# Scan kernel on one core: gate products on GpSimd from a copy of y, maxima joined three to one, and B split in a layout of 128 x 64

## The chip, the cores and the metric

The kernel runs on one core of a Trainium2 chip. Its time is device time in microseconds (us) of one launch; the figure used is the median of three runs. Five engines work in parallel, each through its own queue in order: TensorE (PE, with its weight loads as PEld), VectorE (DVE), ScalarE (ACT), GpSimd (POOL) and SyncE (SP), which here only issues DMAs.

## The reference, cut to what matters

The input x is (16, 96, 64, 64). Two blocks follow each other.

The first block works on windows of 8 x 8 pixels: a 1 x 1 convolution, then for each of the 64 nodes of a window its 9 nearest nodes by cosine distance, then an edge network and a maximum over the neighbours:

```python
feat = concat([x_i, x_j - x_i])                  # K = 9 neighbours j of node i
h = gelu((feat @ ew.T + eb) * es + et)           # O = 192 channels
h = max over the 9 neighbours
y = affine(conv1x1(h, fc2_w, fc2_b), fc2_s, fc2_t) + x
```

The second block is a state space model over the 4096 pixels of an image, in two layers, with D = 192 channels and 16 states:

```python
xs, z = split(layernorm(seq) @ in_w)
xc = silu(causal_conv4(xs));  dt, Bm, Cm = split(xc @ xproj_w)
delta = softplus(dt @ dt_w + dt_b)
h[l] = exp(delta * A) * h[l-1] + delta * Bm[l] * xc[l]    # per channel and state
y = sum over states of h * Cm  +  Dp * xc
seq = seq + (y * silu(z)) @ out_w                          # y * silu(z): "the gate"
```

A fusion product, a normalisation over the batch and the residual end it.

## The kernel before, in words

An image is cut into 8 rows of 512 pixels (a row of 8 windows). An *item* is one row of one layer of one image: 16 x 2 x 8 = 256 items. An item has 8 *steps* p = 0 to 7; each handles two of the 16 states for all 192 channels, as a tile of 128 partitions (64 channels for each of two states) by 3 x 512 columns. A step is

- ACT: `da` = exp(delta * A) in three instructions (L681), made two steps ahead, in one of four buffers `das`;
- PE: `bt`, the row of B of each state spread over 64 partitions by a selection matrix `bsel` (L702). B is held in `bparts` as three bfloat16 parts, whose sum is B;
- DVE: `db` = `u` * `bt` in PSUM (L707), the carry from the row before added into its first column (L852, from `first`), then the scan `hb` (L861);
- POOL: the last state kept (L886), then `hb` = `hb` * C (L887);
- PE: `hb` folded into `y` in PSUM (L718, L720), over all eight steps of the item. `y` has one buffer, in two tiles `ya` (512 columns) and `yb` (256).

All order is written out by hand: a loop over the 2048 steps issues the scan of a step, advances several generators by one yield each, then issues the next `db` and the fold of the step before. Engines follow this order in their queues. The generators, each running beside the steps:

- `norm(n+2)` from p = 0 and `prelude(n+2)` from p = 4 of item n make the inputs of the item after next (`xc`, `z`, `dbl`, `bparts`, `delta`, `u`). In `prelude`, the product `pd` gives dt, B and C in `dbl`; B appears three times in it, in partitions 0, 64 and 96 and up. ACT copies it to `dbl` and as bfloat16 to `bparts` (L612, L613); POOL subtracts (L640), ACT casts the difference (L647), POOL subtracts again (L657). Between these POOL has softplus' sums (L642, L644, L646) and the product for `u` (L652); DMAs then double `delta` and `u` over the partitions (L663, L665). Row C goes to DRAM (L616) and is read back spread over 64 partitions as `ct` (L674).
- `carry(n+1)` from p = 5 makes `first` on POOL and ACT (L690, L692, L696).
- `nearest` (every other item) and `edges` (one over two items) do the first block for later rows. `edges` makes one-hot matrices `oh` (L404 on POOL, L406 and L407 on ACT), products (L438, L441) and gelus (L446) into a buffer of `das`: three tiles of 128 x 512 for a pair of windows. `most` (L382) reduces each over its 8 neighbours; the nodes' own values `sa`, `sb` (L463, L475) join by two maxima (L859), and `fc2` follows (`product` in `edges`).
- `tail(n-1)` at p = 6 multiplies the gated `z` by `out_w` and updates `seq`.

The maxima wait in lists: `most` is put in `later[1]`, two steps on in `between`, and one is taken ahead of a scan where nothing else is, another behind the scan at p = 4 and 5; what is left goes out ahead of the maxima in `late`. The gates of item n-1 are issued on DVE at p = 1 of item n, around the addition of the carry:

```python
acts = opening + (gates(n - 1, y) if p == 1 and n else [])
...
if len(acts) > 1:
    acts.pop(0)()
if k:
    nc.vector.tensor_tensor(db[:, :, 0], db[:, :, 0], carried[n][:, :, p], ALU.add)
for act in acts:
    act()
```

Of the kernel before, what the change touches and what calls it, by code (L numbers as in the profile page):

```python
# [10 lines left out]
F32 = mybir.dt.float32  # L11
# [10 lines left out]
def tile_conv_knn_mamba(ctx: ExitStack, tc: tile.TileContext, w: dict, out: bass.AP):  # L22
# [8 lines left out]
    nc = tc.nc  # L31
# [127 lines left out]
    DT0 = 2 * NS  # L159
    PARTS = (0, 64, 96)  # L160
    ONE0 = PARTS[2] + NS
    bsel = const.tile([128, NPR, 128], BF16, name="bsel")
# [12 lines left out]
    NDA = 4  # L175
    das = [const.tile([128, NB3, Q], F32, name=f"da{i}") for i in range(NDA)]
    zeros = const.tile([128, NB3], F32, name="zeros")
    nc.vector.memset(zeros, 0.0)
# [15 lines left out]
    with tc.tile_pool(name="setup", bufs=2) as sp, tc.tile_pool(name="setup_ps", bufs=2, space=PSUM) as spp:  # L194
        for i in range(NL):
# [34 lines left out]
            nc.vector.memset(xp, 0.0)  # L230
            for r, src, n in ((0, R, 2 * NS), (DT0, 0, R), (PARTS[1], R, NS), (PARTS[2], R, NS)):
                nc.vector.tensor_copy(xp[:, :, r : r + n], xr[:, :, src : src + n])
# [147 lines left out]
    def most(out, g, at):  # L380

        nc.vector.tensor_reduce(out, g, AX.X, ALU.max)  # L382
        if at is not None:
            free.append(at)

    def edges(b, q):
# [4 lines left out]
        for hf in range(2):  # L391
# [29 lines left out]
            if hf == 0:  # L421


                hqa = pr.tile([128, Q], F32, tag="hqa", name=f"hqa_{nm}", bufs=1)
                hqb = pr.tile([128, QH], F32, tag="hqb", name=f"hqb_{nm}", bufs=1)
                hqa4 = hqa.rearrange("p (r w c) -> p w r c", r=WS, w=NW)
                hqb4 = hqb.rearrange("p (r w c) -> p w r c", r=WS, w=NP)


            for p in range(2):  # L430
                ohw = [ohs[p][:, h].rearrange("j i k -> j (i k)") for h in range(2)]
                at = free.popleft()
                g3 = das[at]
                unset.add(at)
                for part in range(3):
                    t = pm.tile([128, Q], F32, tag="mm", name=f"t_{nm}_{hf}_{p}_{part}")
                    if part < 2:
                        nc.tensor.matmul(t, lhsT=vus[p][:, part, :128], rhs=ohw[part], start=True, stop=True)  # L438
                    else:
                        for h in range(2):  # L440
                            nc.tensor.matmul(  # L441
                                t[half(h)], lhsT=vus[p][:, h, 128:], rhs=ohw[h], start=True, stop=True
                            )
                    g = g3[:, part, :]
                    j = part // 2
                    nc.scalar.activation(g, t, AF.Gelu, bias=e_b[:, j : j + 1], scale=e_s[:, j : j + 1])  # L446
                    w2 = 2 * hf + p
                    later[1].append(
                        partial(
                            most,  # L450
                            hqb4[:, w2] if part == 2 else hqa4[:, 2 * w2 + part],
                            g.rearrange("p (r c k) -> p r c k", r=WS, k=KO),
                            at if part == 2 else None,
                        )
                    )
                if p == 0:
                    yield TABLE
            if hf == 1:
# [3 lines left out]
                sa = pr.tile([128, Q], F32, tag="sa", name=f"sa_{nm}", bufs=1)  # L462
                nc.scalar.activation(  # L463
                    sa.rearrange("p (r w c) -> p r w c", r=WS, w=NW),
                    t.rearrange("p (w r c) -> p r w c", r=WS, w=NW),
                    AF.Gelu,
# [5 lines left out]
                for h in range(2):  # L472
                    nc.tensor.matmul(t[half(h)], lhsT=ew1[:, 128:], rhs=y4[:, h], start=True, stop=True)
                sb = pr.tile([128, QH], F32, tag="sb", name=f"sb_{nm}", bufs=1)
                nc.scalar.activation(  # L475
                    sb.rearrange("p (r w c) -> p r w c", r=WS, w=NP),
                    t.rearrange("p (w r c) -> p r w c", r=WS, w=NP),
                    AF.Gelu,
# [6 lines left out]

        late.append(partial(nc.vector.tensor_tensor, hqa, hqa, sa, ALU.max))
        late.append(partial(nc.vector.tensor_tensor, hqb, hqb, sb, ALU.max))
        yield
# [3 lines left out]
        def product():  # L492
            pf = pm.tile([C, Q], F32, tag="mm", name=f"pf2_{nm}")
            nc.tensor.matmul(pf, lhsT=fc2T[:, 0, :], rhs=hqa, start=True, stop=False)
            pf4 = pf.rearrange("o (r p h c) -> o h r p c", r=WS, h=2, c=WS)
            for h in range(2):
                nc.tensor.matmul(
                    pf4[:, h],
                    lhsT=fc2T[:, 1 + h, :],
                    rhs=hqb.rearrange("k (r p c) -> k r p c", r=WS, c=WS),  # L500
                    start=False,
                    stop=False,
                )
            nc.tensor.matmul(pf, lhsT=ident[:C, :C], rhs=xr, start=False, stop=True)
            return pf
# [37 lines left out]
    made = {}  # L543
    carried = {}

    def norm(n):
# [22 lines left out]
    def prelude(n):  # L569
# [5 lines left out]
        xc = pr.tile([128, Q + QH], F32, tag="xc", name=f"xc_{nm}")  # L575
        z = pr.tile([128, Q + QH], F32, tag="z", name=f"z_{nm}", bufs=4)

# [26 lines left out]
        yield  # L604
        bp = bparts[n % 2]
        ps = pm.tile([ONE0, Q], F32, tag="mm", name=f"pd_{nm}")
# [5 lines left out]
        nc.scalar.copy(dbl[:ONE0], ps)  # L612
        nc.scalar.copy(bp[:ONE0], ps)  # L613
        yield
        c_d = dram.tile([NS, Q], F32, tag="c_d", name=f"cd_{nm}")
        nc.sync.dma_start(out=c_d, in_=dbl[NS : 2 * NS, :])  # L616
# [21 lines left out]
        nc.scalar.activation(s1, s1, AF.Identity, bias=neg1)  # L638

        nc.gpsimd.tensor_tensor(dbl[PARTS[1] : ONE0], dbl[PARTS[1] : ONE0], bp[PARTS[1] : ONE0], ALU.subtract)  # L640
        yield
        nc.gpsimd.tensor_tensor(e, e, s1, ALU.subtract)  # L642
        yield
        nc.gpsimd.tensor_tensor(ln, ln, e, ALU.add)  # L644
        yield
        nc.gpsimd.tensor_tensor(ln, ln, rl, ALU.add)  # L646
        nc.scalar.copy(bp[PARTS[1] : ONE0], dbl[PARTS[1] : ONE0])  # L647
        yield
# [6 lines left out]
        doubled(u, s1)  # L655

        nc.gpsimd.tensor_tensor(bp[PARTS[2] : ONE0], dbl[PARTS[2] : ONE0], bp[PARTS[2] : ONE0], ALU.subtract)  # L657

# [51 lines left out]
    def folded(n, p, hb, y):  # L710

        i = items[n][1]
        xc = made[n][0]
        if p == 0:
            nc.tensor.matmul(y[0], lhsT=dp_diag[i][:, 0, :], rhs=xc[:, :Q], start=True, stop=False)
            nc.tensor.matmul(y[1], lhsT=dp_diag[i][:, 1, :], rhs=xc[:, Q:], start=True, stop=False)
        for h in range(2):
            nc.tensor.matmul(y[0][half(h)], lhsT=fold, rhs=hb[:, h, :], start=False, stop=(p == NPR - 1))  # L718
        for h in range(2):
            nc.tensor.matmul(  # L720
                y[1][half(h)], lhsT=fold, rhs=hb[:, 2, bass.ts(h, QH)], start=False, stop=(p == NPR - 1)
            )

    def gates(n, y):
        z = made[n][1]
        return [
            partial(nc.vector.tensor_tensor, z[:, cols], z[:, cols], part, ALU.mult)
            for cols, part in zip((slice(0, Q), slice(Q, Q + QH)), y)
        ]

    def tail(n):
# [3 lines left out]
        seq = seqs[b, k]  # L735
        z = made[n][1]

        def product():
            po = pm.tile([C, Q], F32, tag="mm", name=f"pow_{nm}")
            nc.tensor.matmul(po, lhsT=out_w[i][:, 0, :], rhs=z[:, :Q], start=True, stop=False)  # L740
            for h in range(2):
                nc.tensor.matmul(
                    po[:, bass.ts(h, QH)], lhsT=out_w[i][:, 1 + h, :], rhs=z[:, Q:], start=False, stop=False
                )
            nc.tensor.matmul(po, lhsT=ident[:C, :C], rhs=seq, start=False, stop=True)
            return po

# [67 lines left out]
    for m, (n, p) in enumerate(order):  # L815
# [27 lines left out]
        while uses:  # L843
            uses.pop(0)()
        acts = opening + (gates(n - 1, y) if p == 1 and n else [])
        opening.clear()
# [14 lines left out]
        nc.vector.tensor_tensor_scan(*(t.rearrange("p c q -> p (c q)") for t in (hb, das[at], db)), 0.0, ALU.mult, ALU.add)  # L861
        free.append(at)
        if p == 6 and n:
            going.append(tail(n - 1))
# [13 lines left out]
        if behind is not None:  # L878
            if p == 1:
                y = [  # L880
                    py.tile([128, Q], F32, tag="ya", name=f"ya_{nm}"),
                    py.tile([128, QH], F32, tag="yb", name=f"yb_{nm}"),
                ]
# [3 lines left out]
        nc.gpsimd.tensor_tensor(hb, hb, ct.unsqueeze(1).to_broadcast([128, NB3, Q]), ALU.mult)  # L887
        behind = (n, p, hb)
        while not held and len(soon) < AHEAD and coming:
            ahead()  # L890
    folded(*behind, y)
    for act in gates(NI - 1, y):
        act()
    drain(*going, tail(NI - 1))
# [50 lines left out]
```

## Time and profile before

| what | value |
| --- | --- |
| median of 3 runs | 13199.09 us (13182.12 to 13199.22) |
| span of the profiled execution | 13206.7 us |
| DVE busy | 12215.5 us, 92% |
| POOL busy | 11455.2 us, 87% |
| PE busy | 11033.5 us, 84% |
| ACT busy | 10512.7 us, 80% |
| mean granted TensorE clock | 0.959 |
| DMA, share of 16 engines in the SP queue | 33.1% |

The profiled execution has no time of its own beside its span; the span is 7.6 us (0.06%) over the median of the runs. In a group line the columns are line, engine, operation, output <- input, shapes and count, then busy us and mean ns of one, then the idle time of the engine ahead of them and who ended it. In a timeline line they are start, duration, engine, line, operation, tiles and shapes; in brackets stands the idle time ahead of it and its releaser.

### The profile page before, as it was taken

The numbers are of one execution on the slowest core, as the hardware profiler recorded it, in microseconds if no ns is written. First come the engines' busy times: TensorE is split into PE (matmuls) and PEld (weight loads), VectorE is DVE, ScalarE is ACT, GpSimd is POOL, SyncE is SP. The second block draws the span as 40 slices with busy tenths as digits, with TensorE's granted clock in tenths as the row PEclk, the third lists the DMA queues.
The fourth block names the chain that finished last, engine by engine and source line by source line (L and its number), as shares of the span: only waits on it lengthen the run. The fifth ranks groups of instructions, "written<-read, shape, count | busy, mean of one in ns | idle before, by whom it ended". The sixth has DMA issues, their size and how long they took to land.

```text
span 13206.7 us, 155165 instructions
## 1 busy us (share of the span) xinstructions
PE 11033.5 (84%) x46663; PEld 4408.0 (33%) x46664; DVE 12215.5 (92%) x9981; ACT 10512.7 (80%) x16401; POOL 11455.2 (87%) x7591
## 2 busy tenths in 40 slices
PE   6788888888888888888888888888888888888871
PEld 2233333333333333333333333333333333333320
DVE  2699999999999999999999999999999999999993
ACT  4688888888888888888888888888888888888762
POOL 1798999989999999999999899999999999998881
PEclk8899999999999999999999999999999999999985
DMA  1233333333333333333333333333333333333337
GB/s 27 72 86 91 91 91 86 92 91 86 92 88 93 87 90 94 89 88 91 91 90 87 91 92 87 90 92 91 85 94 89 90 88 90 93 88 90 84 89 237
DMA packets 887099, 1205.74 MB, mean 91 GB/s; under 512 B 282272, under 2 KB 413742, under 8 KB 877040
## 3 DMA queue, kind: packets, MB, share of 16 engines
q1 hardware_dynamic: 871792, 1169.34, 33.1%
q10 hardware_dynamic: 14464, 26.48, 0.6%
q8 instruction: 367, 6.01, 0.2%
q14 instruction: 476, 3.90, 0.1%
HBM read 706.82 MB, written 85.72 MB: 60 GB/s over the span
## 4 chain that ended last, share of the span: by engine, by line
DVE 30%; POOL 19%; PE 18%; ACT 14%; DMA 7%; issue 7%; SPq 4%; POOLq 0%; DVEq 0%; ACTq 0%
DVE hb L861 18%; POOL hb L887 12%; DVE db L707 9%; ACT da L681 5%; PE ya L718 3%; DMA ct<-cd 2%; SPq L663 2%; PE t L441 2%; PE t L438 1%; PE pj L584 1%; SPq L665 1%; PE yb L720 1%; PE bt L702 1%; PE pdta L622 1%; SPq L674 1%
## 5 line engine op out<-in xcount | busy, mean ns | idle before, releaser
L887 POOL TENSOR_TENSOR hb<-hb,ct 128x1536 f32<-128x1536 f32 x2048 | 7069.8, 3452 | 388.7 <-PE yb L720 87.9
L861 DVE TENSOR_TENSOR_SCAN hb<-da,db 128x1536 f32<-128x1536 f32 x2048 | 6859.6, 3349 | 108.3 <-ACT da L681 20.0
L681 ACT ACTIVATE da<-delta,a 128x511 f32<-128x511 f32 x6144 | 3940.0, 713 | 67.8 <-DVE hb L861 59.1
L707 DVE TENSOR_TENSOR db<-u,bt 128x1536 f32<-128x1536 f32 x2048 | 3602.9, 1759 | 170.0 <-PE pdtb L625 47.4
L718 PE MATMUL ya<-hb,fold 128*64 128x512 f32 x8192 | 2248.8, 628 | 220.9 <-POOL hb L887 215.2
L446 ACT ACTIVATE da<-t,eb,es 128x512 f32<-128x512 f32 x1536 | 1173.1, 777 | 778.9 <-PE t L438 518.7
L702 PE MATMUL bt<-bparts,bsel 128*128 128x512 bf16 x2047 | 797.5, 390 | 806.7 <-DVE db L707 745.8
L720 PE MATMUL yb<-hb,fold 128*64 128x256 f32 x8192 | 1265.6, 388 | 0.0
L720 PEld LDWEIGHTS yb<-hb,fold 128*64 128x64 f32 x8192 | 604.2, 141 | 1231.5 <-issue 1231.5
L438 PE MATMUL t<-oh,vu 128*128 128x512 f32 x2048 | 993.2, 607 | 23.3 <-ACT da L446 23.3
L584 PE MATMUL pj<-hn,conv_in 128*128 128x512 f32 x2048 | 930.9, 597 | 9.8 <-POOL hn L567 9.8
L718 PEld LDWEIGHTS ya<-hb,fold 128*64 128x64 f32 x8192 | 491.0, 139 | 1313.9 <-issue 552.2
L404 POOL TENSOR_SCALAR oh<-idb,node 64x1024 f32<-64x1024 uint16 x256 | 731.2, 2856 | 131.1 <-DMA idb<-idxd 131.1
L886 POOL COPY state<-hb 128x3 f32<-128x3 f32 x1792 | 342.1, 191 | 571.7 <-DVE hb L861 428.1
L441 PE MATMUL t<-oh,vu 128*64 128x512 f32 x2048 | 572.1, 638 | 302.1 <-ACT da L446 299.0
L382 DVE TENSOR_REDUCE hqa<-da 128x64 f32<-128x512 f32 x1024 | 677.0, 671 | 149.2 <-ACT da L446 149.1
L415 PE MATMUL pv<-ewT,y 96*64 96x192 f32 x2048 | 458.9, 349 | 248.6 <-ACT rs L564 166.0
L438 PEld LDWEIGHTS t<-oh,vu 128*128 128x128 f32 x2048 | 395.7, 195 | 465.3 <-issue 265.9
L596 ACT ACTIVATE xc<-pj,conv_b 128x512 f32<-128x512 f32 (+1 forms) x512 | 297.6, 581 | 289.6 <-PE pj L589 183.6
L584 PEld LDWEIGHTS pj<-hn,conv_in 128*128 128x128 f32 x2048 | 395.7, 193 | 395.0 <-issue 374.5
L589 PE MATMUL pj<-hn,conv_in 128*64 128x256 f32 x4096 | 498.9, 385 | 0.0
L415 PEld LDWEIGHTS pv<-ewT,y 96*64 96x64 f32 x2048 | 246.2, 140 | 696.9 <-ACT rs L564 268.6
(188 smaller groups left out, 18447.0 us busy)
## 6 DMA issues: line engine op xcount, KB each, us to landing
ct<-cd SPq DMA_DIRECT2D x4096, 128.0 KB
delta<-ln SPq DMA_DIRECT2D x1024, 128.0 KB
u<-s SPq DMA_DIRECT2D x1024, 128.0 KB
idb<-idxd SPq DMA_DIRECT2D x256, 256.0 KB
delta<-ln SPq DMA_DIRECT2D x1024, 64.0 KB
u<-s SPq DMA_DIRECT2D x1024, 64.0 KB
x<-in_x SPq DMA_DIRECT2D x128, 192.0 KB
rn<-r4d SPq DMA_DIRECT2D x128, 192.0 KB
```

The lines of the kernel that those rows point to most:

```text
L404: nc.gpsimd.tensor_scalar(ohj, numbers, node, None, ALU.is_equal)
L438: nc.tensor.matmul(t, lhsT=vus[p][:, part, :128], rhs=ohw[part], start=True, stop=True)
L441: nc.tensor.matmul(t[half(h)], lhsT=vus[p][:, h, 128:], rhs=ohw[h], start=True, stop=True)
L446: nc.scalar.activation(g, t, AF.Gelu, bias=e_b[:, j : j + 1], scale=e_s[:, j : j + 1])
L584: nc.tensor.matmul(ps, lhsT=wt[:, t, :128], rhs=hn[:, off : off + Q], start=(t == 0), stop=(t == taps - 1))
L681: nc.scalar.activation(da[:, c, 1:Q], delta[:, c, 1:], AF.Exp, scale=a_neg[i][:, c, p : p + 1])
L702: nc.tensor.matmul(bt, lhsT=bsel[:, p, :], rhs=made[n][2], start=True, stop=True)
L707: nc.vector.tensor_tensor(db, made[n][5], bt.unsqueeze(1).to_broadcast([128, NB3, Q]), ALU.mult)
L718: nc.tensor.matmul(y[0][half(h)], lhsT=fold, rhs=hb[:, h, :], start=False, stop=(p == NPR - 1))
L720: nc.tensor.matmul(y[1][half(h)], lhsT=fold, rhs=hb[:, 2, bass.ts(h, QH)], start=False, stop=(p == NPR - 1))
L861: nc.vector.tensor_tensor_scan(*(t.rearrange("p c q -> p (c q)") for t in (hb, das[at], db)), 0.0, ALU.mult, ALU.add)
L887: nc.gpsimd.tensor_tensor(hb, hb, ct.unsqueeze(1).to_broadcast([128, NB3, Q]), ALU.mult)
```

## The change

**Gates.** `y` becomes one tile of 128 x 2 x 512. Behind the scan at p = 1, ACT copies 768 columns of it from PSUM to a buffer of a ring of four `zs`; behind the product of that step, one POOL instruction of 128 x 768 multiplies the copy by `z`. `tail` reads the copy. The two DVE products go.

**Maxima.** The three reductions of 512 columns of a window pair become one of 1536, and the two maxima with `sa` and `sb` become one of 768. The result `hq` keeps the order of windows, and `fc2` reads it with other strides, in five products instead of four.

**B's parts.** `pd` holds B once. A DMA lays B's 16 rows of 512 out as 128 rows of 64; POOL makes the three bfloat16 parts there in five instructions; three DMAs put them in `bparts`. The two ACT casts and the two POOL subtractions go.

```diff
-    PARTS = (0, 64, 96)
-    ONE0 = PARTS[2] + NS
+    PARTS = (0, 32, 64)
+    ONE0 = DT0 + R
+    SEG = 128 // NS
+    QS = Q // SEG
...
+    zs = deque(const.tile([128, Q + QH], F32, name=f"z{i}") for i in range(4))
...
     def most(out, g, at):
-        nc.vector.tensor_reduce(out, g, AX.X, ALU.max)
-        if at is not None:
-            free.append(at)
+        nc.vector.tensor_reduce(out, g.rearrange("p s (i k) -> p s i k", k=KO), AX.X, ALU.max)
+        free.append(at)
...
-                    w2 = 2 * hf + p
-                    later[1].append(
-                        partial(
-                            most,
-                            hqb4[:, w2] if part == 2 else hqa4[:, 2 * w2 + part],
-                            g.rearrange("p (r c k) -> p r c k", r=WS, k=KO),
-                            at if part == 2 else None,
-                        )
-                    )
+                later[1].append(partial(most, hq[:, 2 * hf + p], g3, at))
...
-        late.append(partial(nc.vector.tensor_tensor, hqa, hqa, sa, ALU.max))
-        late.append(partial(nc.vector.tensor_tensor, hqb, hqb, sb, ALU.max))
+        late.append(partial(nc.vector.tensor_tensor, hq, hq, sa, ALU.max))
...
+            nc.tensor.matmul(pf, lhsT=ident[:C, :C], rhs=xr, start=True, stop=False)
+            pf5 = pf.rearrange("o (r w h c) -> o h w r c", r=WS, h=2, c=WS)
             for h in range(2):
+                for part, wt in ((h, 0), (2, 1 + h)):
+                    nc.tensor.matmul(
+                        pf5[:, h],
+                        lhsT=fc2T[:, wt, :],
+                        rhs=hq[:, :, part].rearrange("k w (r c) -> k w r c", c=WS),
...
         nc.scalar.copy(dbl[:ONE0], ps)
-        nc.scalar.copy(bp[:ONE0], ps)
         yield
+        bs = pr.tile([128, QS], F32, tag="bs", name=f"bs_{nm}", bufs=1)
+        nc.sync.dma_start(out=bs, in_=dbl[:NS, :])
...
-        nc.gpsimd.tensor_tensor(dbl[PARTS[1] : ONE0], dbl[PARTS[1] : ONE0], bp[PARTS[1] : ONE0], ALU.subtract)
+        b3 = pr.tile([128, 3, QS], BF16, tag="b3", name=f"b3_{nm}")
+        for part in range(3):
+            nc.gpsimd.tensor_copy(b3[:, part], bs)
+            if part < 2:
+                nc.gpsimd.tensor_tensor(bs, bs, b3[:, part], ALU.subtract)
         yield
+        bp = bparts[n % 2]
+        for r, part in zip(PARTS, range(3)):
+            nc.sync.dma_start(out=bp[r : r + NS], in_=b3[:, part])
...
-        nc.scalar.copy(bp[PARTS[1] : ONE0], dbl[PARTS[1] : ONE0])
...
-        nc.gpsimd.tensor_tensor(bp[PARTS[2] : ONE0], dbl[PARTS[2] : ONE0], bp[PARTS[2] : ONE0], ALU.subtract)
...
+    def emptied(n, y):
+        yc = zs.popleft()
+        nc.scalar.copy(yc, y.rearrange("p s q -> p (s q)")[:, : Q + QH])
+        return yc
+
+    def gate(n, yc):
         z = made[n][1]
-        return [
-            partial(nc.vector.tensor_tensor, z[:, cols], z[:, cols], part, ALU.mult)
-            for cols, part in zip((slice(0, Q), slice(Q, Q + QH)), y)
-        ]
+        nc.gpsimd.tensor_tensor(yc, yc, z, ALU.mult)
+        zs.append(z)
+        gated[n] = yc
...
-        acts = opening + (gates(n - 1, y) if p == 1 and n else [])
+        acts = list(opening)
...
         free.append(at)
+        if p == 1 and n:
+            yc = emptied(n - 1, y)
...
         nc.gpsimd.tensor_tensor(hb, hb, ct.unsqueeze(1).to_broadcast([128, NB3, Q]), ALU.mult)
+        if p == 1 and n:
+            gate(n - 1, yc)
```

More of the change, by code (lines that the diff above doesn't have):

```diff
@@ L230, in tile_conv_knn_mamba @@
             nc.vector.memset(xp, 0.0)
-            for r, src, n in ((0, R, 2 * NS), (DT0, 0, R), (PARTS[1], R, NS), (PARTS[2], R, NS)):
+            for r, src, n in ((0, R, 2 * NS), (DT0, 0, R)):
                 nc.vector.tensor_copy(xp[:, :, r : r + n], xr[:, :, src : src + n])
@@ L421, in edges @@
             if hf == 0:
[L424 to L427, printed above, removed]
+                hq = pr.tile([128, NP, NB3, NN], F32, tag="hq", name=f"hq_{nm}", bufs=1)
             for p in range(2):
@@ L461, in edges @@
                 nc.tensor.matmul(t, lhsT=ew1[:, :128], rhs=y, start=True, stop=True)
-                sa = pr.tile([128, Q], F32, tag="sa", name=f"sa_{nm}", bufs=1)
+                sa = pr.tile([128, NP, NB3, NN], F32, tag="sa", name=f"sa_{nm}", bufs=1)
                 nc.scalar.activation(
-                    sa.rearrange("p (r w c) -> p r w c", r=WS, w=NW),
-                    t.rearrange("p (w r c) -> p r w c", r=WS, w=NW),
+                    sa[:, :, 0:2],
+                    t.rearrange("p (w h i) -> p w h i", w=NP, h=2),
                     AF.Gelu,
@@ L473, in edges @@
                     nc.tensor.matmul(t[half(h)], lhsT=ew1[:, 128:], rhs=y4[:, h], start=True, stop=True)
[L474 removed]
                 nc.scalar.activation(
[L476 to L477 removed]
+                    sa[:, :, 2],
+                    t.rearrange("p (w i) -> p w i", w=NP),
                     AF.Gelu,
@@ L493, in product @@
             pf = pm.tile([C, Q], F32, tag="mm", name=f"pf2_{nm}")
-            nc.tensor.matmul(pf, lhsT=fc2T[:, 0, :], rhs=hqa, start=True, stop=False)
-            pf4 = pf.rearrange("o (r p h c) -> o h r p c", r=WS, h=2, c=WS)
+            nc.tensor.matmul(pf, lhsT=ident[:C, :C], rhs=xr, start=True, stop=False)
+            pf5 = pf.rearrange("o (r w h c) -> o h w r c", r=WS, h=2, c=WS)
             for h in range(2):
[L497 to L504, printed above, removed]
+                for part, wt in ((h, 0), (2, 1 + h)):
[3 more added lines that the diff above has]
+                        rhs=hq[:, :, part].rearrange("k w (r c) -> k w r c", c=WS),
+                        start=False,
+                        stop=h == 1 and part == 2,
+                    )
             return pf
@@ L544, in tile_conv_knn_mamba @@
     carried = {}
+    gated = {}
     def norm(n):
@@ L575, in prelude @@
         xc = pr.tile([128, Q + QH], F32, tag="xc", name=f"xc_{nm}")
-        z = pr.tile([128, Q + QH], F32, tag="z", name=f"z_{nm}", bufs=4)
+        z = zs.popleft()
         def project(wt, taps, part, out, bias):
@@ L604, in prelude @@
         yield
-        bp = bparts[n % 2]
         ps = pm.tile([ONE0, Q], F32, tag="mm", name=f"pd_{nm}")
@@ L714, in folded @@
         if p == 0:
-            nc.tensor.matmul(y[0], lhsT=dp_diag[i][:, 0, :], rhs=xc[:, :Q], start=True, stop=False)
-            nc.tensor.matmul(y[1], lhsT=dp_diag[i][:, 1, :], rhs=xc[:, Q:], start=True, stop=False)
+            nc.tensor.matmul(y[:, 0], lhsT=dp_diag[i][:, 0, :], rhs=xc[:, :Q], start=True, stop=False)
+            nc.tensor.matmul(y[:, 1, :QH], lhsT=dp_diag[i][:, 1, :], rhs=xc[:, Q:], start=True, stop=False)
         for h in range(2):
-            nc.tensor.matmul(y[0][half(h)], lhsT=fold, rhs=hb[:, h, :], start=False, stop=(p == NPR - 1))
+            nc.tensor.matmul(y[half(h), 0], lhsT=fold, rhs=hb[:, h, :], start=False, stop=(p == NPR - 1))
         for h in range(2):
             nc.tensor.matmul(
-                y[1][half(h)], lhsT=fold, rhs=hb[:, 2, bass.ts(h, QH)], start=False, stop=(p == NPR - 1)
+                y[half(h), 1, :QH], lhsT=fold, rhs=hb[:, 2, bass.ts(h, QH)], start=False, stop=(p == NPR - 1)
             )
-    def gates(n, y):
+    def emptied(n, y):
[3 more added lines that the diff above has]
+    def gate(n, yc):
         z = made[n][1]
-        return [
-            partial(nc.vector.tensor_tensor, z[:, cols], z[:, cols], part, ALU.mult)
-            for cols, part in zip((slice(0, Q), slice(Q, Q + QH)), y)
-        ]
+        nc.gpsimd.tensor_tensor(yc, yc, z, ALU.mult)
+        zs.append(z)
+        gated[n] = yc
     def tail(n):
@@ L735, in tail @@
         seq = seqs[b, k]
-        z = made[n][1]
+        z = gated.pop(n)
         def product():
@@ L745, in product @@
             nc.tensor.matmul(po, lhsT=ident[:C, :C], rhs=seq, start=False, stop=True)
+            zs.append(z)
             return po
@@ L879, in tile_conv_knn_mamba @@
             if p == 1:
[L880 to L883, printed above, removed]
+                y = py.tile([128, 2, Q], F32, tag="y", name=f"y_{nm}")
             folded(*behind, y)
@@ L891, in tile_conv_knn_mamba @@
     folded(*behind, y)
-    for act in gates(NI - 1, y):
-        act()
+    gate(NI - 1, emptied(NI - 1, y))
     drain(*going, tail(NI - 1))
```

## The prediction

> **What bounds the kernel now.** The page first: busy time by engine, then the costliest groups.
>
> ```profile
> PE 11033.5 (84%) x46663; PEld 4408.0 (33%) x46664; DVE 12215.5 (92%) x9981; ACT 10512.7 (80%) x16401; POOL 11455.2 (87%) x7591
> ...
> L887 POOL TENSOR_TENSOR hb<-hb,ct 128x1536 f32<-128x1536 f32 x2048 | 7069.8, 3452 | 388.7 <-PE yb L720 87.9
> L861 DVE TENSOR_TENSOR_SCAN hb<-da,db 128x1536 f32<-128x1536 f32 x2048 | 6859.6, 3349 | 108.3 <-ACT da L681 20.0
> ...
> L707 DVE TENSOR_TENSOR db<-u,bt 128x1536 f32<-128x1536 f32 x2048 | 3602.9, 1759 | 170.0 <-PE pdtb L625 47.4
> ```
>
> 2048 steps of scan plus product make 10.46 ms of the 12.2 ms of DVE. In the windows view DVE is 96.4% busy between 2400 and 12000 us (9253.06 of 9600), POOL 91.2%, PE 86.8%, ACT 83.1%. The groups that the change touches, from the groups kept apart by shape, DVE then POOL:
>
> ```profile
> L382 DVE TENSOR_REDUCE hqa<-da 128x64 f32<-128x512 f32 x1024 | 677.0, 671 | 149.2 <-ACT da L446 149.1
> L859 DVE TENSOR_TENSOR hqa<-hqa,sa 128x512 f32<-128x512 f32 x122 | 105.3, 863 | 0.0
> ```
> ```profile
> L642 POOL TENSOR_TENSOR e<-e,s 128x768 f32<-128x768 f32 x256 | 465.5, 1818 | 12.0 <-ACT s L638 11.7
> L657 POOL TENSOR_TENSOR bparts<-dbl,bparts 16x512 bf16<-16x512 f32 x256 | 297.0, 1160 | 20.1 <-POOL first L690 0.2
> ```
>
> Then the timeline of DVE at an even item's start:
>
> ```profile
> 6011.03 3.35 DVE L861 TENSOR_TENSOR_SCAN hb<-da,db 128x1536 f32<-128x1536 f32 x1
> 6014.47 1.76 DVE L707 TENSOR_TENSOR db<-u,bt 128x1536 f32<-128x1536 f32 x1
> 6016.34 0.17 DVE L852 TENSOR_TENSOR db<-db,first 128x3 f32<-128x3 f32 x1
> 6016.61 3.35 DVE L861 TENSOR_TENSOR_SCAN hb<-da,db 128x1536 f32<-128x1536 f32 x1
> 6020.07 1.76 DVE L707 TENSOR_TENSOR db<-u,bt 128x1536 f32<-128x1536 f32 x1
> 6022.95 0.69 DVE L850 TENSOR_TENSOR z<-z,ya 128x512 f32<-128x512 f32 x1 [1.12 <-PE ya L718]
> ...
> 6023.96 3.35 DVE L861 TENSOR_TENSOR_SCAN hb<-da,db 128x1536 f32<-128x1536 f32 x1
> ```
>
> A bare step takes 5.5 us: 5.28 of work and 0.25 of gaps between dependent instructions. The step with the gates takes 7.35, with 1.12 of waiting for y. I number a row's 16 steps (two items) 0 to 15 from the even item's p = 0, and average scan starts over 94 rows of the trace (steps 256 to 1760): a row takes 98.1 us, a bare step 5.53, step 1 (gates) 7.44, step 9 (gates) 6.42 where its like without gates takes 5.55, step 4 (one reduction) 5.94, steps 5 and 6 (two each) 6.24, step 7 (one) 5.87, step 13 6.36, step 14 (four and both maxima with sa, sb) 8.61. DVE sets the pace; the others' queues decide how much of a DVE saving shows.
>
> **The change on DVE, per row.** Gates: 7.44 - 5.53 at step 1 and 6.42 - 5.55 at step 9 go: -2.78 us, the wait included.
>
> Joined maxima: rows give 139 ns for a reduction of 8 columns (L521) and 671 for 512, so 1.06 ns per column and 1.75 us for 1536; three cost 2.01 now. But the three are spread over steps where they fill gaps: one adds only 5.94 - 5.53 = 0.41 to a step, not 0.67. The even item's six cost 0.41 + 0.71 + 0.71 + 0.34 = 2.17; two joined ones, each filling one gap (0.27), cost 2 x 1.48 = 2.97. The odd item's six and its two maxima cost 6.36 + 8.61 - 2 x 5.53 = 3.91; two joined ones 2.97, and one maximum of 768 columns. That takes 0.96 by L771's quiet rows (0.69 for 512, 0.42 for 256), and I add the 0.17 by which L859 exceeds them: 1.13, less 0.28 of gap, 0.85; together 3.82. Joining costs +0.7: fewer busy us, more of them in the way. DVE in all: -2.05 a row, -262 us over 128 rows.
>
> L859's two-input maximum is mostly 0.68 us, but up to 2.39 while POOL runs. The Trainium skill (SBUF — State Buffer, "Who interferes with whom") says a DVE instruction with two SBUF inputs contends with a GpSimd instruction reading SBUF, and that the loser waits it out. By that, one maximum could lose up to 3.45 us, an estimate that L887's row prices; the measured mean surcharge is what the sum uses.
>
> **On POOL, per item.** The gate is L642's shape: 1.82 and a 0.08 gap, behind product hb of p = 1, ahead of step 2's work. L640 and L657 go (1.16 each, 0.16 of gaps). Five instructions of 128x64 come. The trace has no such copy: from below 0.19 (state, 3 columns), from above 1.16 (L657, bfloat16, 512 columns). For a subtraction I interpolate 0.23 (24 columns, L690) and 1.82 (768 columns): 0.32; for a copy 0.25, between that and 0.19. With gaps 1.78, bounds 1.0 and 6.2. Net +1.2 an item, 2.4 a row. POOL's waits over 0.2 us are 6.6 a row now, so it fits on average; what counts is when.
>
> The gate's POOL row is 1.65 times the two DVE rows (0.69 + 0.41). The Trainium skill (GPSIMD Engine Reference, "Engine selection") speaks against elementwise products on GpSimd, about twice as slow. By that 2.2 us, an estimate, and a row 0.8 heavier on POOL. The sum takes the row.
>
> I follow POOL's backlog, from a scan's end to its product's start: each step adds POOL's work and subtracts DVE's period, with 0.29 as floor. Done for the kernel before, this gives the trace's means (step 0 1.87, step 3 3.27, step 6 0.68, step 14 0.29). The new work of POOL at steps 0 to 15, gaps included (each product's group in its trace, with the changes above; the gate falls into the groups of steps 2 and 10): 6.66, 5.75, 8.56, 7.33, 5.46, 4.04, 5.11, 6.69, 5.62, 5.75, 8.48, 5.38, 5.43, 3.8, 3.7, 6.54, in all 94.3. Against DVE's new periods (5.53 at steps 0 and 1, 5.51, with the waits found below 6.51 and 7.17, then 7.02, 5.53) the backlog becomes: step 15 1.3, step 0 2.4, step 1 2.6, step 2 5.7, step 3 6.5, step 4 4.8, step 5 1.8, step 6 1.4; in the odd item step 10 5.3, and the floor at 13 and 14.
>
> **What is late next.** (a) Broadcast bt. On PE it stands behind fold and edge products:
>
> ```profile
> 6026.75 0.38 PE L415 MATMUL pv<-ewT,y 96*64 96x192 f32 x1 [1.37 <-ACT rs L564]
> ...
> 6030.48 0.39 PE L702 MATMUL bt<-bparts,bsel 128*128 128x512 bf16 x1
> ```
> ```profile
> 6024.19 1.93 ACT L681 ACTIVATE da<-delta,a 128x511 f32<-128x511 f32 x3
> 6026.02 0.67 ACT L564 ACTIVATE rs<-pvar,eps_t 96x512 f32<-96x512 f32 x1
> ```
>
> ACT's new copy of y (0.80 by 0.60 and 0.39 for 512 and 256 columns from PSUM, L629) stands just ahead of rs. y is ready 2.4 to 2.8 us before ACT gets there, so no wait for PE is added, but all behind it (rs, pv, fold, bt, the gelus) comes 0.8 later. bt of step 3 is now ready 1.89 before its use; DVE is 1.91 earlier and bt 0.80 later: DVE waits 0.82, about 0.15 more at step 4 (slack 1.84), 0.2 at steps 12 and 13. ACT's removed casts (0.58, 0.61) lie where ACT waits or behind the gelus: nothing.
>
> (b) Carry. L852 of p = 0 needs first, which POOL makes behind oh:
>
> ```profile
> 6012.56 2.85 POOL L404 TENSOR_SCALAR oh<-idb,node 64x1024 f32<-64x1024 uint16 x1
> 6015.39 0.21 POOL L696 TENSOR_TENSOR first<-first,state 128x12 f32<-128x12 f32 x1
> ```
>
> It ends 0.75 before L852 here; at step 8 the mean slack is 0.72, some rows 0.03. Backlog at step 6 rises from 0.68 to 1.4 and step 7 loses its reduction (0.34): a wait of about 0.35 a row. At step 0 the backlog is back at its floor: nothing.
>
> Moves of little price: SP gets one bs and three bparts DMAs an item, some 0.6 us of issue each, ahead of ct loads for two steps later; they wait for POOL work that precedes product hb of p = 0, so those loads are not the last. fc2's product has the same columns in five matmuls instead of four. The z ring has a buffer for y's copy; its release, the gate, lies four steps ahead of its next use. The opening and the final pass are untouched; the last item's copy and gate end 1.5 us later, once.
>
> Sum: 98.1 - 2.05 + 0.82 + 0.15 + 0.2 + 0.35 = 97.55, -0.53 a row, -68 us. The profiled span is 13206.7, 0.06% above the median, 13199; 13199 - 68 = 13131.
>
> **Rivals.** Cover holds: bt and first are not waited for (ACT reaches y's copy in idle time). Then the whole 2.05 shows: 12937. For: ACT idles 17%; against: the rows above show it solid at that place.
>
> Slower, by the carry: if POOL is heavier than I think, first decides. At 0.45 instead of 0.28 per small instruction the backlog at step 6 is 2.3 and the wait 1.15; with 0.3 at bt of step 13, the row is 98.4, 13246. It decides from a backlog of about 2.0 at step 6.
>
> POOL as bound: at 1.16 for each small instruction a row on POOL grows from 94.3 to 103 us; 13830. Only L657's row speaks for it, with eight times the columns.
>
> The gain is just eaten, within 0.2%: the terms cancel.
>
> **Numbers.** About 0.2%, 26 us, is what a measurement of this kernel can tell from no change. Chances: my sum 0.45 (own range 13050 to 13190), cover holds 0.18, cancelled 0.09, carry 0.24, POOL bound 0.04. Faster: 0.18 and most of the 0.45, 0.57; the band 0.18; slower 0.25, most of the carry case and POOL bound. The range, 12950 to 13270, reaches into both neighbours.
>
> **What would show it.** DVE busy near 11700; joined reductions near 1.75 us; L850's wait gone; step 1 down to 5.5; a wait for bt at step 3, one for first at step 8; POOL's small instructions near 0.3; its product hb starting 5 to 6.5 us behind the scan at steps 2 and 3. Small instructions over 0.5, or hb's scan waiting for folds, would make the forecast wrong upward; no wait for bt, downward.

## The result, and the profile after

The changed kernel takes 13302.61 us (median of 4, 13293.32 to 13317.68) against 13197.71 before: ratio 1.0081, 95% interval 1.0069 to 1.0093. The forecast was 13131, faster; it is 105 us slower, above the range. The profiled span is 13291.5 against 13206.7.

The page after, busy line and costliest groups:

```profile
PE 11202.6 (84%) x46920; PEld 4335.0 (33%) x46920; DVE 12172.1 (92%) x8313; ACT 10384.2 (78%) x16145; POOL 11604.0 (87%) x8615
...
L885 POOL TENSOR_TENSOR hb<-hb,ct 128x1536 f32<-128x1536 f32 x2048 | 7072.0, 3453 | 373.3 <-DVE hb L860 141.7
L860 DVE TENSOR_TENSOR_SCAN hb<-da,db 128x1536 f32<-128x1536 f32 x2048 | 6862.1, 3351 | 157.9 <-ACT da L674 20.1
L700 DVE TENSOR_TENSOR db<-u,bt 128x1536 f32<-128x1536 f32 x2048 | 3607.6, 1762 | 387.5 <-PE bt L695 201.6
```

DVE's busy time fell by only 43 us (12215.5 before), where the gates alone were 281; and db now waits for bt. Busy time counts instructions that overlap once: added up one by one, DVE's instructions take 256 us less (gates -281, reductions -141, maxima +157, the rest +9), and 213 us by which the short ones overlapped their neighbours are gone. All engines' shares stand within 2 points of before, so no share shows where the time went. The groups by shape do, first of DVE, then of POOL:

```profile
L385 DVE TENSOR_REDUCE hq<-da 128x192 f32<-128x1536 f32 x512 | 890.7, 1740 | 173.2 <-ACT da L445 173.2
L858 DVE TENSOR_TENSOR hq<-hq,sa 128x768 f32<-128x768 f32 x122 | 314.2, 2576 | 0.0
...
L770 DVE TENSOR_TENSOR hq<-hq,sa 128x768 f32<-128x768 f32 x6 | 5.7, 942 | 0.0
```
```profile
L725 POOL TENSOR_TENSOR z<-z,z 128x768 f32<-128x768 f32 x256 | 466.5, 1822 | 2.9 <-ACT z L720 2.9
...
L631 POOL CAST b<-bs 128x64 bf16<-128x64 f32 x768 | 182.5, 238 | 62.2 <-DMA bs<-dbl 29.4
...
L633 POOL TENSOR_TENSOR bs<-bs,b 128x64 f32<-128x64 f32 x512 | 157.3, 307 | 41.2
```

Durations were forecast well but for one: the joined maximum takes 2.58 us beside the steps (L858), 0.94 in the quiet opening (L770), where I had 1.13. The durations of the maximum, min, median and max, from the views by source line, first the kernel before (its 512 columns), then after:

```profile
L859 DVE TENSOR_TENSOR hqa<-hqa,sa x122: 679/684/2385, 510.3 to 12378.0; 128x512 f32<-128x512 f32 x122
```
```profile
L858 DVE TENSOR_TENSOR hq<-hq,sa x122: 2412/2621/2704, 506.7 to 12465.9; 128x768 f32<-128x768 f32 x122
```

Step 14 of the kernel before, on DVE, with three reductions (x2 and x1) between the carry's addition and the maximum:

```profile
6001.65 0.17 DVE L852 TENSOR_TENSOR db<-db,first 128x3 f32<-128x3 f32 x1
6001.73 1.27 DVE L382 TENSOR_REDUCE hqa<-da 128x64 f32<-128x512 f32 x2
6002.91 0.68 DVE L382 TENSOR_REDUCE hqb<-da 128x64 f32<-128x512 f32 x1
6003.51 1.72 DVE L859 TENSOR_TENSOR hqa<-hqa,sa 128x512 f32<-128x512 f32 x1
```

After, the same place has none of them; the timelines of DVE and POOL there:

```profile
5939.71 3.34 DVE L860 TENSOR_TENSOR_SCAN hb<-da,db 128x1536 f32<-128x1536 f32 x1
5943.15 1.76 DVE L700 TENSOR_TENSOR db<-u,bt 128x1536 f32<-128x1536 f32 x1
5944.95 0.17 DVE L851 TENSOR_TENSOR db<-db,first 128x3 f32<-128x3 f32 x1
5945.03 2.42 DVE L858 TENSOR_TENSOR hq<-hq,sa 128x768 f32<-128x768 f32 x1
```
```profile
5943.19 3.46 POOL L885 TENSOR_TENSOR hb<-hb,ct 128x1536 f32<-128x1536 f32 x1 [2.28 <-PE pj L574]
```

POOL's product ends at 5946.65, the maximum at 5947.45: the product's end plus a quiet maximum's 0.94, less a head start of 0.14. In all 122 cases the maximum starts while a product runs and ends 0.81 to 0.82 us after it. It counts as busy time, so no wait is listed.

Step durations, from the scan starts, averaged over the same 94 rows as in the prediction (us; steps 0 to 15, then the row); "predicted" is put together from the prediction's terms:

```
step            0    1    2    3    4    5    6    7    8    9   10   11   12   13   14   15   row
before       5.53 7.44 5.51 5.69 5.94 6.24 6.24 5.87 5.63 6.42 5.55 5.81 5.69 6.36 8.61 5.55 98.10
predicted    5.53 5.53 5.51 6.51 7.17 7.02 5.53 5.53 5.98 5.55 5.55 5.81 5.79 8.60 6.38 5.55 97.55
after        5.54 5.49 5.52 6.80 7.09 6.94 5.50 5.52 5.64 5.54 5.58 5.90 5.94 8.44 7.82 5.55 98.81
```

Step 14 is 1.4 over the forecast, the whole row 1.26.

### The profile page after: what moved, and what is told of

The parts are those of the page before. It is cut to its first block, busy times and chain, and to the rows that moved or that the text cites. A ratio compares the mean times of both kernels' runs of the same rounds, so it can differ in the third digit from the quotient of the medians.

```text
span 13291.5 us, 155856 instructions
## 1 busy us (share of the span) xinstructions
PE 11202.6 (84%) x46920; PEld 4335.0 (33%) x46920; DVE 12172.1 (92%) x8313; ACT 10384.2 (78%) x16145; POOL 11604.0 (87%) x8615
## 4 chain that ended last, share of the span: by engine, by line
POOL 26%; DVE 23%; PE 17%; ACT 13%; issue 10%; DMA 6%; SPq 4%; ACTq 0%; POOLq 0%; DVEq 0%
POOL hb L885 15%; DVE hb L860 14%; DVE db L700 8%; ACT da L674 5%; PE y L711 3%; POOL ln L640 2%; PE pj L574 2%; SPq L656 2%; DMA ct<-cd 2%; PE y L713 1%; SPq L658 1%; PE pj L579 1%; POOL hn L557 1%; POOL e L638 1%; PE bt L695 1%
## 5 line engine op out<-in xcount | busy, mean ns | idle before, releaser
L700 DVE TENSOR_TENSOR db<-u,bt 128x1536 f32<-128x1536 f32 x2048 | 3607.6, 1762 | 387.5 <-PE bt L695 201.6
L711 PE MATMUL y<-hb,fold 128*64 128x512 f32 x8192 | 2280.9, 636 | 294.5 <-POOL hb L885 285.5
L713 PE MATMUL y<-hb,fold 128*64 128x256 f32 x8192 | 1268.2, 389 | 0.0
L385 DVE TENSOR_REDUCE hq<-da 128x192 f32<-128x1536 f32 x512 | 890.7, 1740 | 173.2 <-ACT da L445 173.2
L713 PEld LDWEIGHTS y<-hb,fold 128*64 128x64 f32 x8192 | 608.4, 142 | 1252.3 <-issue 1252.3
L711 PEld LDWEIGHTS y<-hb,fold 128*64 128x64 f32 x8192 | 491.4, 140 | 1355.2 <-issue 560.9
L708 PE MATMUL y<-xc,dp_diag 128*128 128x512 f32 x512 | 375.5, 824 | 165.4 <-ACT z L720 165.4
```

The lines of the kernel that those rows point to most:

```text
L385: nc.vector.tensor_reduce(out, g.rearrange("p s (i k) -> p s i k", k=KO), AX.X, ALU.max)
L700: nc.vector.tensor_tensor(db, made[n][5], bt.unsqueeze(1).to_broadcast([128, NB3, Q]), ALU.mult)
L711: nc.tensor.matmul(y[half(h), 0], lhsT=fold, rhs=hb[:, h, :], start=False, stop=(p == NPR - 1))
L713: nc.tensor.matmul(y[half(h), 1, :QH], lhsT=fold, rhs=hb[:, 2, bass.ts(h, QH)], start=False, stop=(p == NPR - 1))
```

## The experiments

Ratios are to the kernel before on the same chip, with 95% intervals; "row" is the 94-row mean. DVE's waits for bt in three kernels, one line each (us in all, times, the longest): after, then the first experiment, then the fifth. The last two include one wait of about 47 us in the opening, which after lists under another name; without it they are 312 and 263.

```profile
DVE db L700 <- PE bt L695: 201.6, 200, 3.9
```
```profile
DVE db L700 <- PE bt L695: 359.1, 222, 47.0
```
```profile
DVE db L704 <- PE bt L699: 310.2, 229, 46.8
```

**1. The maximum moved behind the scan of step 13.**

```diff
         if between and p in (4, 5):
             between.popleft()()
+        elif late and p == 5:
+            late.pop(0)()
```

> The changed kernel with one line moved: the joined maximum of hq and sa is issued right behind the scan of the odd item's p = 5, ahead of the next db, where POOL stands idle, and no longer ahead of the scan of p = 6. Theory (it waits out a POOL product that began 1.64 us before it): it takes 0.95 us instead of 2.58, step 14 falls from 7.82 to about 6.2, 1.6 us a row, and the time goes from 13303 to about 13110, below the kernel before. Rival (bt, late behind ACT's copy of y, and POOL's backlog take what DVE gains): the maximum may get shorter, but the time stays within 30 us of 13303.

Measured: 13202.59, ratio 1.0004 (0.9995 to 1.0014), level with before. The maximum's group, from the view of tile hq:

```profile
L878 DVE TENSOR_TENSOR hq<-hq,sa x122: 930/931/935, 503.3 to 12375.7; 128x768 f32<-128x768 f32 x122
```

It starts with the scan's end, ahead of POOL's next product, and never waits (min, median and max within 5 ns). Where the product starts inside the maximum, 0.22 us behind its start (30 of 122 cases), the product pays: 4.0 us instead of 3.45. Step 14 falls from 7.82 to 6.20 as expected, but step 3 rises from 6.80 to 7.67: 0.87 of 1.62 returns as a wait for bt (201.6 and 312 us in all, by the lines above). Both theories were half right. The prediction set only the gain at step 1 ("DVE is 1.91 earlier") against bt's slack; a gain at step 14 counts there too, since bt's chain moves up with only part of it: ACT reaches its copy of y 15.5 us after the scan of step 15 here, 14.6 in after.

**2. Gates back on DVE, from y in PSUM; all else as after.** 

```diff
-        acts = list(opening)
+        acts = opening + (gates(n - 1, y) if p == 1 and n else [])
...
-            yc = emptied(n - 1, y)
...
-            gate(n - 1, yc)
```

> The changed kernel with the gates back on DVE as two products from y in PSUM; joined maxima and B's parts stay. Theory (the gate's move is worth having, the maxima are what costs): steps 1 and 9 get 2.8 us a row longer, the waits for bt at steps 3, 4 and 12, about 1.6 us a row, go: about 1.2 us a row, 13303 to about 13450. Rival (the gate on POOL and its copy on ACT are what made the change slower): 13250 or less.

Measured: 13539.85, ratio 1.0262 (1.0245 to 1.0279), row 100.77. More than the 13450 expected: against these gates, with joined maxima, the gate's move is worth 1.8%, so it did not make the change slow. Steps 1 and 9 are 7.40 and 7.20, step 3 is 5.70. But these gates read y as the one tile that the change made of it: each waits for the folds into both parts, where the first gate before waited for `ya` alone. DVE waits for y 1.18 us a row at step 1 and 0.83 at step 9, against 0.75 and 0.19 in number 4 and 0.95 and 0.35 in number 8, both with two tiles. So 0.7 to 1.1 of the 1.96 us a row may be the tile's, an estimate from these waits; it was not separated.

**3. Reductions kept apart.** `most` reduces 512 columns into its part of `hq`; the rest as after.

```diff
-                later[1].append(partial(most, hq[:, 2 * hf + p], g3, at))
+                    later[1].append(partial(most, hq[:, 2 * hf + p, part], g, at if part == 2 else None))
```

> The changed kernel with the three reductions of a window pair kept apart (each of 512 columns into its part of hq); the maximum with sa stays joined, the gate stays on POOL. Theory: single reductions fill gaps, 0.7 us a row; three of them ahead of the maximum let POOL's product end first, so that the maximum falls from 2.58 to about 1.2 us: about 2.1 us a row, 13303 to about 13035. Rival (a joined reduction saves the fixed part of two, 0.27 us of 2.01): 512 times 0.27, slower by about 137 us, 13440; and if only the maximum's collision counts, about 13125.

Measured: 13169.01, ratio 0.9980 (0.9970 to 0.9989), row 97.86. Steps 4 to 7 take 24.35 together against after's 25.05: three spread reductions are 0.7 a row cheaper than joined ones, as priced. The maximum falls to 1.20 (beside the steps), since three reductions ahead of it let most of POOL's product pass. Of that gain step 3 takes back 0.4, steps 8 and 11 0.3 and 0.2, so half of the expected 268 us came.

**4. B's parts alone, on the kernel before**: of the change's diff, the hunks of `PARTS`, `bs`, `b3` and `bp`.

```diff
-        nc.scalar.copy(bp[:ONE0], ps)
+        nc.sync.dma_start(out=bs, in_=dbl[:NS, :])
```

> The kernel before with only B's parts made in 128 rows of 64 columns. Theory: POOL loses 0.6 us an item net and ACT 1.2, but DVE sets the pace, so 13198 becomes 13160 to 13198. Rival (four more DMAs an item with pieces of 128 and 256 bytes, and SP waiting for POOL, hold up ct): slower by 30 us or more.

Measured: 13140.66, ratio 0.9957 (0.9940 to 0.9973), row 97.54: a little more than expected. Step 1 falls from 7.44 to 6.98 (bt is ready there 0.44 sooner, and DVE's wait for y falls from 1.21 to 0.75) and step 14 from 8.61 to 8.43; step 9 rises by 0.14. At step 14 the maximum of 512 columns falls from 0.863 to 0.691, its quiet value: POOL no longer has L657 ahead of the product of step 13, whose backlog falls from 0.80 to 0.33. Why step 1 gains was not separated; ACT's cast behind `dbl`, gone now, is the nearest cause.

**5. Three edits together:** reductions apart, the joined maximum behind the scan of step 14, and ACT's copy of y between the two `rs` of `norm`. The first is number 3's diff; the others, cut to what matters (`pending` holds the call of `emptied`, put in behind the scan at p = 1):

```diff
-        while late:
-            if between:
-                between.popleft()()
-            else:
-                late.pop(0)()
+        while late and between:
+            between.popleft()()
...
+        if late and p == 6:
+            late.pop(0)()
         if after is not None:
...
         nc.scalar.activation(rs, ps, AF.Ln, bias=eps_t[:C], scale=1.0 / C)
+        while pending:
+            pending.pop(0)()
         nc.scalar.activation(rs, rs, AF.Exp, scale=-0.5)
```

> The changed kernel with three edits: reductions kept apart in threes, the joined maximum behind the scan of the odd item's p = 6, and ACT's copy of y between rs = Ln and rs = Exp of norm instead of ahead of both. Theory (bt of step 3 hangs on ACT's rs, which frees the PSUM buffer for pv, and on the copy; either may go first): against the variant with three reductions alone (13169, row 97.86), step 3 goes from 7.20 to about 6.5, steps 14 and 15 fall by 0.9 together, of which about half returns as a wait at step 3: about 1.1 us a row, 13030, below the kernel before by over 1%. Rival (all that DVE gains ahead of step 3 comes back there as a wait for bt, whatever the order on ACT): 13140 to 13170.

Measured: 13068.09, ratio 0.9896 (0.9879 to 0.9912), the fastest of all, over 1% below both kernels. Row 97.12. Less than the 13030 expected: steps 14 and 15 fall by 0.6 together against number 3, not 0.9, and step 3 falls to 5.92, but step 4 rises from 6.00 to 6.94.

**6. After with that copy's place alone changed** (the last hunk of number 5).

> The changed kernel with ACT's copy of y between rs = Ln and rs = Exp of norm, and nothing else. Theory (the 0.78 us copy ahead of rs is what makes bt late at step 3): step 3 falls from 6.80 to about 6.1, 90 us, 13303 to about 13215. Rival (POOL's backlog of 5 us at step 2 holds the fold ahead of bt): step 3 stays at 6.8 and the time within 20 us of 13303.

Measured: 13294.49, ratio 1.0070 (1.0054 to 1.0087): no change from after. Step 3 falls by more than expected, 6.80 to 5.76, and step 4 rises from 7.09 to 7.69, step 11 from 5.90 to 6.43. The wait moved on: bt of step 3 is ready 1.7 us sooner, counted from the scan of step 15, but bt of step 4 as late as before (26.3 us behind that scan, 26.2 in after), though the gelus ahead of it come 0.4 sooner. Neither theory had this; what holds bt of step 4 was not separated.

**7. The gate alone, on the kernel before**: of the change's diff, the hunks of `zs`, `emptied` and `gate`, with y as one tile.

```diff
-        acts = opening + (gates(n - 1, y) if p == 1 and n else [])
+        acts = list(opening)
...
+            yc = emptied(n - 1, y)
...
+            gate(n - 1, yc)
```

> The kernel before with only the gates moved to POOL, from ACT's copy of y; maxima and B's parts as before. Theory (DVE gains 2.8 us a row at steps 1 and 9, and nearly all of it returns as waits for bt, as ACT's copy delays it): 13150 to 13230. Rival (the sum on record: 2.78 gained, 0.8 to 1.2 returned): 1.6 to 2.0 us a row, about 12970.

Measured: 13352.58, ratio 1.0116 (1.0099 to 1.0133), slower than either theory. Steps 1 and 9 gain 2.8; step 3 rises from 5.69 to 7.82, step 8 by 0.41, step 14 from 8.61 to 9.62. The maximum of 512 columns, from the groups by shape:

```profile
L867 DVE TENSOR_TENSOR hqa<-hqa,sa 128x512 f32<-128x512 f32 x122 | 229.5, 1881 | 0.0
```

The mean was 0.863 before. POOL's backlog at step 13 is 1.96 instead of 0.80, so its product ends later, and the maximum with it.

**8. The joined maxima alone, on the kernel before**: of the change's diff, the hunks of `most`, `hq`, `late` and `pf5`.

```diff
-        late.append(partial(nc.vector.tensor_tensor, hqa, hqa, sa, ALU.max))
-        late.append(partial(nc.vector.tensor_tensor, hqb, hqb, sb, ALU.max))
+        late.append(partial(nc.vector.tensor_tensor, hq, hq, sa, ALU.max))
```

> The kernel before with only the maxima joined. Theory (0.7 us a row for lost gaps in the even item, 1.4 for a maximum that always waits out POOL's product, and the gates' wait for y longer by about 1 as DVE comes to them sooner or PE later): 2.1 to 3.2 us a row, 13470 to 13600. Rival (the sum on record: 0.7 us a row): 13290.

Measured: 13476.69, ratio 1.0208 (1.0191 to 1.0225), row 100.27, 2.2 over before: steps 4 to 7 +0.65, steps 13 and 14 +1.36, step 9 +0.35, step 12 +0.12, step 1 -0.25. As the theory for this run had it, and against 0.7 in the prediction.

**9. After with ACT's copy cut to 3 columns.**

```diff
-        nc.scalar.copy(yc, y.rearrange("p s q -> p (s q)")[:, : Q + QH])
+        nc.scalar.copy(yc[:, :NB3], y.rearrange("p s q -> p (s q)")[:, :NB3])
```

> The changed kernel with ACT's copy of y cut from 768 columns to 3 (the ring zs is set to zero once at the start), so the gate's product has no y in it; all instructions and their order stay. Theory (ACT's time ahead of rs, pv and the gelus is what makes bt late): ACT loses 0.58 us an item; the waits at step 3 (1.1 us), 4, 11 and 12 (0.5 together) shrink by about 1.0 us a row: 13303 to about 13175. Rival (POOL's backlog, or PE's own order, holds bt): within 30 us of 13303.

Measured: 13272.22, ratio 1.0041 (1.0026 to 1.0055), 0.4% below after where 1% was expected. Step 3 falls by 0.86 to 5.94: bt there hangs on ACT. But step 8 rises by 0.36, steps 10 and 12 by 0.2 each. At step 8 the waits name the carry:

```profile
DVE db L853 <- POOL first L691: 57.9, 97, 1.6
```

In after the same wait is 7.1 us, 14 times.

**10. After with POOL's gate cut to 3 columns.**

```diff
-        nc.gpsimd.tensor_tensor(yc, yc, z, ALU.mult)
+        nc.gpsimd.tensor_tensor(yc[:, :NB3], yc[:, :NB3], z[:, :NB3], ALU.mult)
```

> The changed kernel with POOL's gate product cut from 768 columns to 3, so that most of y's copy goes ungated; ACT's copy stays whole. Theory (bt hangs on ACT and PE, not on POOL): POOL loses 1.6 us an item and its backlog at steps 2 and 3 falls from 5 to about 3.5, but step 3 stays near 6.8, step 14 near 7.8 and the time within 40 us of 13303. Rival (POOL is the bound now): 1 to 2 us a row, 13050 to 13170.

Measured: 13294.74, ratio 1.0057 (1.0040 to 1.0074), 0.2% below after and within the theory's 40 us. The backlog at step 2 falls from 5.08 to 3.46; step 3 stays (6.94) and step 14 too (7.82). POOL's 1.6 us do not hold bt.

**11. Number 5 without its last hunk**, the copy's new place.

> The changed kernel with the reductions kept apart in threes and the joined maximum behind the scan of the odd item's p = 6; ACT's copy of y stays ahead of rs. Theory (moving the copy behind Ln only moves the wait from step 3 to steps 4 and 11): 13060 to 13110, beside 13068 with the copy moved. Rival (with the maximum out of the way the copy's place counts for its 0.7 us a row): about 13155.

Measured: 13094.07, ratio 0.9904 (0.9888 to 0.9921); row 97.15, as the theory had it. The copy's place only moves the wait: steps 3 and 4 take 7.20 and 6.02 here, 5.92 and 6.94 in number 5.

**12. B's parts, gates on DVE, the two old maxima behind the scan of step 14** (number 4's edit and this one).

```diff
+        while late and p == 6:
+            late.pop(0)()
         if after is not None:
```

> The kernel before with B's parts changed and its two maxima behind the scan of the odd item's p = 6; gates on DVE, reductions in threes. Theory (maxima that start with the scan's end, ahead of POOL's product, meet no product and fill gaps): steps 14 and 15 fall by about 0.5 together, 13141 to about 13080. Rival (what DVE gains there comes back at step 1 as a wait for y): 13125 to 13145.

Measured: 13300.29, ratio 1.0057 (1.0040 to 1.0074), a miss on both theories. The view of tile hqb shows why:

```profile
L879 DVE TENSOR_TENSOR hqb<-hqb,sb x122: 415/418/3681, 514.1 to 12483.5; 128x256 f32<-128x256 f32 x122
```

The first maximum is quiet (0.67), but the second, 0.6 us behind it, finds POOL's product just begun in 30 of 122 cases and waits it out whole: up to 3.68, in the mean 1.21. These are the image's last rows, where POOL keeps no state ahead of the product. One joined maximum has no such second start. Steps 14 and 15 together take 0.56 more than in number 4 (14.54 against 13.98), steps 1 and 9 0.74 more: DVE's waits for y grow from 114 to 179 us in all, those for bt by 29; what makes y late was not separated.

**13. Number 11 with the gates on DVE** (number 2's diff).

> The variant with three reductions and the joined maximum behind the scan of p = 6 (0.990 of before), with the gates back on DVE. Theory (out of the maximum's way the gate's move saves 2.8 us a row at steps 1 and 9 and loses about 2.5 of it to bt at step 3, the carry at step 8 and waits at 11 and 12): 0.3 us a row slower or even, 0.990 to 0.994 of before. Rival (the gate's move is what gains): 2 us a row or more slower, 1.006 of before or above.

Measured: 13161.76, ratio 0.9972 (0.9961 to 0.9982), between both. With the maximum out of the way the gate's move is worth 0.7% against these gates: 97.76 against 97.15 a row. Steps 1 and 9 gain 3.1, step 3 gives back 1.5, the rest lies at 4, 8, 12 and 13. Here too y is one tile. DVE's wait for y at step 1, in number 4 and then here:

```profile
DVE z L855 <- PE ya L723: 90.6, 82, 1.6
```
```profile
DVE z L845 <- PE y L714: 147.9, 120, 2.3
```

That is 0.45 us a row more, and step 9 has 0.1 more: together nearly the 0.61. Whether the gate's move gains anything over gates that read y in two tiles is not shown.

## Why the prediction was wrong, point by point

- **The step that failed** is "and I add the 0.17 by which L859 exceeds them". A mean surcharge of mostly quiet cases (0.68, up to 2.39) was carried over to an instruction at another place in POOL's rhythm. Before, three reductions stood between the carry's addition and the maximum, and 49 of 122 maxima met no product at all; after, nothing stands there, so every maximum starts some 1.8 us ahead of the product's end and pays 1.63 instead of 0.17. So the maximum took 2.58 where the sum had 1.13, and step 14 is 1.44 over, more than the whole row's miss of 1.26; the other steps make up 0.2 between them. The Trainium skill's rule (SBUF — State Buffer, "Who interferes with whom"), which I set beside the row and left out of the sum, describes what happened: the loser waits for the whole instruction. Numbers 1 and 12 show that who starts first decides.
- **Gates:** step 1 7.44 to 5.49, step 9 6.42 to 5.54, as forecast.
- **Joined reductions:** 1.740 us against 1.75, and 0.7 a row dearer in the even item (number 3), as forecast.
- **bt at step 3:** 1.11 over before against 0.82 forecast. That bt hangs on ACT is confirmed (number 9 takes 0.86 of it away, number 10 nothing), but the term was too small, since it set only step 1's saving against bt's slack: a third to a half of what numbers 3 and 1 save at steps 13 and 14 returns there as well. Number 1, the forecast's case without the collision, waits 1.98 there. This is the second step that failed: without the collision the change is level with before, not 68 us faster. Of the miss of 171 us number 1 takes away 100; what is left, 0.53 a row, is less than the 1.16 by which this wait exceeds its term. The granted TensorE clock, 0.952 after and 0.959 before, does not explain the wait: in number 9 it is 0.950, and the wait at step 3 is 0.25.
- **Carry at step 8:** 0.35 was forecast, nothing came, since the backlog at step 6 was 0.60 and not 1.4, with a longer step 3 and POOL's sums a little high. It came where the backlog was higher: 1.30 and a wait of 0.47 in number 9, 1.57 and 0.53 in number 7.
- **POOL:** 0.24 and 0.31 for the small instructions (0.25 and 0.32), backlog 5.1 and 5.6 at steps 2 and 3 (5.7 and 6.5). The rival "POOL as bound" is refuted by number 10.
- **DVE busy** was to fall to 11700 and is 12172. The collision gives back 176 us (122 times 1.45), and the overlap of the short instructions, 213 us, was left out; by the prediction's own prices the figure would have been about 11780, an estimate.
- **Small slips of the sum:** it mixes -2.05 and -2.07 for DVE (97.57 as written, 3 us of the whole), and the carry rival's row of 98.4 makes 13237, not 13246.
- **Engine Selection:** the Trainium skill (GPSIMD Engine Reference, "Engine selection") would keep the gate on VectorE. Here the move costs 1.2% on the kernel before (7) and gains 0.7 and 1.8% over gates that read y as one tile (13, 2), of which part, or all in 13, may be the tile's. The row is 1.82 against 1.10 on DVE; what the move is worth went by what stands beside it.

The three parts alone give -0.4, +2.1 and +1.2%, together +0.8%: they are not additive, since each lengthens or shortens the same waits. What else orders the chain of PE and ACT ahead of step 3, beyond ACT's copy, is not settled; the fastest variant still waits for bt, most at steps 4 (1.09 us a row) and 11 (0.52).

## What to carry to other kernels

A mean duration hides a bimodal one: where a group's maximum is several times its median, price the instruction at its new place against what the other engine runs at that moment, not at the mean. Here the DVE instruction with two SBUF inputs belonged right behind the scan that releases POOL's next product (numbers 1, 11), as one instruction, not two (12). And a saving counts only up to the next chain: check how much earlier the consumer may come before it waits, at every place where the saving lands.

## What was not expected of the hardware

A joined reduction can cost more than three: three of 0.67 us spread over steps add 1.1 (six add 2.17 to steps 4 to 7 before), because independent instructions fill the gaps of about 0.1 us around dependent ones and overlap their neighbours by 0.08 (in the lines of after above the maximum starts at 5945.03, the addition ends at 5945.12), while one of 1.74 adds 1.4 to 1.5 (two add 2.91 to step 13 after). And the maximum's wait for POOL's product appears nowhere as idle time: L858's 200 us over its quiet time (122 x 1.63) stand in DVE's busy time.
